# Means over heads by column tiles, squared once and spread by row tiles, in a two-layer convolution kernel

## The chip, the cores and the metric

The kernel runs on one core of one Trainium2 chip. The metric is the device time of one execution in microseconds (us). Ten runs of the kernel before took 4981.3 to 4992.86 us, median 4985.96. Engines: TensorE (PE; its weight loads are PEld), VectorE (DVE), ScalarE (ACT), GpSimd (POOL) and SyncE (SP), which only issues transfers here.

## The reference, cut to what matters

Layer 0 takes 32 images of 128 channels, 56 x 56 pixels: a depthwise convolution, a normalisation, and a mixture of eight experts of which each pixel uses two. Layer 1 then works on its result:

```python
feat = gelu(batchnorm(conv2d(x, conv_w, padding=3, dilation=3)))     # 64 channels
F2 = fft2(feat)
qkv = F2.reshape(B, 8 heads, 8 channels, N)
q = complex_l2_norm(qkv); k = complex_l2_norm(qkv); v = qkv
attn = einsum('bhdn,bhen->bhde', q, conj(k)) * tau
attn = complex(softmax(attn.real), softmax(attn.imag))
out_f = abs(ifft2(einsum('bhde,bhen->bhdn', attn, v)))
cg = sigmoid(conv1x1(gelu(batchnorm(conv1x1(F2.real)))))
gate = abs(ifft2(cg * F2))
return concatenate([out_f, gate], axis=1) + x
```

The kernel uses that out_f needs no transform at all: a matrix that mixes channels commutes with the transform, the real part of the attention acts on feat as a real 8 x 8 matrix per head, and the softmax of the imaginary part, which is constant, gives the mean over the eight channels of the head. So out_f is the root of (attn x feat) squared plus (mean over the head of feat) squared. That second term has only one row per head, but every channel of the head needs it.

## The kernel before, in words

Layer 0 ends with the experts; they write rows of `yf` in device memory. Layer 1 then goes over 16 pairs of images. The 128 partitions of a pair hold the 64 channels of one image and the 64 of the other, so there are 16 heads of 8 partitions.

Layer 0's result has still to be brought together for each pixel: 1568 indirect transfers, issued by POOL (line 400, in `release`), gather 128 rows of `yf` each into tiles `y` of seven (six buffers). When the 14 gathers of a row block are in, `total` (line 416) adds its two `y` to `xa` on DVE, writes the sum out on SP's queue, and `bring` (line 439) reads it back as `xs`. There are seven row blocks and so 98 gathers to a pair. A gather can start when its `y` has been added, and `y` is added where `total` stands in DVE's order. `worked(w)` sets that place: each piece of TensorE work reports its columns w, and one gather is asked for per `PACE` of them; `total` follows a block's last gather by seven. `bring` asks for whatever is still missing.

For a pair, `front` places the row blocks (`place`: seven transposes on PE, tile `pxs`, four additions on DVE, line 1174) and does the dilated convolution in seven groups of 8 rows (448 columns): `pf`, line 1185, nine taps in three steps of three, the two images side by side in two tiles of 64 columns. `back` does the rest: a forward transform of feat (tiles `pt`, `mid`, `pm`; line 1228 transposes, line 1215 copies, line 1236 multiplies), the attention matrix, the second forward transform into `Z`, then the stage that is edited, then two inverse transforms.

The edited stage: for each of the seven groups g, `attend(g)` multiplies feat by attn into a bank `pre` (line 1325) and by `meanw`, a 128 x 128 matrix with blocks of 1/8, into a bank `pim` (line 1326), so that each channel receives the mean of its head. ACT squares both (lines 1328 and 1329), DVE adds them back into feat (line 1330). Between the groups the gate is worked out: `pq` (line 1351, four column tiles of 32), and `pq2` (line 1363, four row tiles of 32 with a bank each), then the sigmoid (line 1369) and the product with Z on DVE (line 1374). `attended` takes the root later, between the steps of the inverse transform.

Banks: a pool of five serves `pre`, `pim`, `pq`, `pq2`, `pt`, `pm` and `pxs`; `pf` has two of its own.

Order: the front of the next pair is mixed into the back of this one by columns. After each piece of `back`, front steps are written until this goal is met:

```python
goal = max(0, made - LEAD) * FRONT // (MAIN - LEAD)
if w < 0:
    goal = max(goal, fed - w * 3 * 8 * W)
```

`made` counts the columns of back so far (a transform's step 64 per transpose and its output columns, an attend 896, each half of the gate 464), a front step counts 1344 (three taps) or 448 (a placed block), MAIN is 31304, FRONT 31360, LEAD a sixth of MAIN. A yield of -1 or -2 forces that many steps of taps. Over a pair back reports 27720 columns (MAIN also has 3584 of the gram matrix that are not reported), front 31360. The last pair has no front to mix in. On top of this, the framework's scheduler settles each engine's order when the program is built: by its own costs it pulls later work forward where it sees an engine waiting. The trace shows this where the taps of one step stand in pieces of two and four between `pt` and `pm`.

Of the kernel before, what the change touches and what calls it, by code (L numbers as in the profile page):

```python
# [30 lines left out]
F32 = mybir.dt.float32  # L31
I32 = mybir.dt.int32
AF = mybir.ActivationFunctionType
ALU = mybir.AluOpType
# [10 lines left out]
NT = H // 2  # L45
# [3 lines left out]
KF = 29  # L49
NPIX = H * W  # L50
P8 = 8
NB = H // P8
# [22 lines left out]
def conv_seq_kernel(ctx: ExitStack, tc: tile.TileContext, t: dict, out: bass.AP, dbg: dict):  # L75
    nc = tc.nc
# [14 lines left out]
    def bank(name):  # L91
        return psum.tile([128, 512], F32, tag="bank", name=name)

    def load(pool, name, shape, src, eng=None):
        s = pool.tile(shape, F32, name=name, tag=name)
        (eng or nc.sync).dma_start(out=s, in_=src)
        return s
# [24 lines left out]
    with tc.tile_pool(name="a1", bufs=1) as a1, tc.tile_pool(name="a2", bufs=2) as a2, tc.tile_pool(  # L122
        name="a4", bufs=4
    ) as a4, tc.tile_pool(
        name="a5", bufs=5
# [252 lines left out]
    step = {}  # L378
# [92 lines left out]
    if True:  # L471
# [39 lines left out]
        for u in range(U):  # L511
            nc.vector.tensor_scalar(
                out=blocks[:, u, :], in0=iota[:R, :NC], scalar1=float(-u), scalar2=None, op0=ALU.add
# [4 lines left out]
            out=token, in0=iota[:R], scalar1=-128.0, scalar2=lane[:R], op0=ALU.add, op1=ALU.add  # L518
# [601 lines left out]
    d1 = ctx.enter_context(tc.tile_pool(name="d1", bufs=1))  # L1120
    d2 = ctx.enter_context(tc.tile_pool(name="d2", bufs=2))
# [29 lines left out]
    gsc, gbi = batchnorm("cgbn")  # L1151
    tau = load(d1, "tau", [128, 1], t["tau"])
    neg = load(d1, "neg", [128, 128], t["neg"])
    meanw = load(d1, "meanw", [128, 128], t["meanw"])
    rw = load(d1, "rw", [2 * W, 4 * KF], t["rw"])
    rh = load(d1, "rh", [2 * H, 4 * KF], t["rh"])
    ih = load(d1, "ih", [4 * KF, 2 * H], t["ih"])
# [95 lines left out]
    def back(pr, xps, feat):  # L1253
# [56 lines left out]
        for i, w in enumerate(  # L1310
# [6 lines left out]
                parts[i]()  # L1317
            yield w

        def attend(g):  # L1320

            pre = bank("pre")
            pim = bank("pim")
            ftf = feat[:, 8 * g * W : 8 * (g + 1) * W]
            nc.tensor.matmul(pre[:, : 8 * W], lhsT=attn, rhs=ftf, start=True, stop=True)  # L1325
            step["pe"] = nc.tensor.matmul(pim[:, : 8 * W], lhsT=meanw, rhs=ftf, start=True, stop=True)
            sr = d2.tile([128, 8 * W], F32, name="sr")
            nc.scalar.activation(sr, pre[:, : 8 * W], AF.Square)
            nc.scalar.activation(pim[:, : 8 * W], pim[:, : 8 * W], AF.Square)
            nc.vector.tensor_tensor(out=ftf, in0=sr, in1=pim[:, : 8 * W], op=ALU.add)  # L1330
            return 2 * 8 * W

        def attended(g):

# [11 lines left out]
        NQ4 = NK * K2  # L1346
        starts = [min(q * NK, KF - NK) for q in range(4)]
        yield attend(0)
        pq = bank("pq")
        for q, k0 in enumerate(starts):  # L1350
            nc.tensor.matmul(
                pq[32 * q : 32 * (q + 1), :NQ4], lhsT=g1, rhs=Z[:, k0 : k0 + NK, :K2], start=True, stop=True,
                tile_position=(0, 32 * q),
# [3 lines left out]
        yield NQ4  # L1357
        for g in (1, 2, 3):
            yield attend(g)
        pq2 = [bank("pq2") for k0 in starts]  # L1360
        for q in range(4):
            p = slice(32 * q, 32 * (q + 1))
            nc.tensor.matmul(
                pq2[q][:, :NQ4], lhsT=g2[p, :], rhs=c1_[p, :], start=True, stop=True,
                tile_position=(32 * q, 0),
            )
        for q, k0 in enumerate(starts):
# [7 lines left out]
                out=zq, in0=zq, in1=gt[:, new:].broadcast_to([128, NK - new, 2, K2]), op=ALU.mult  # L1375
            )
        yield NQ4
        for g in range(4, NB):
            yield attend(g)
        yield -2  # L1380


# [34 lines left out]

    MAIN = 2 * (NT * (64 + 4 * KF) + KF * (64 + 4 * KF)) + NT * 128 + NB * 16 * W + 2 * -(-KF // 4) * 2 * KF  # L1420
    FRONT = NB * (NB * 64 + 9 * 8 * W)
    LEAD = MAIN // 6
    PACE = (MAIN + FRONT) / (2 * NP) * 1.07

# [6 lines left out]
    for pr in range(NI // 2):  # L1431
        then, steps = None, iter(())
        if pr + 1 < NI // 2:
            then = pair(pr + 1)
            steps = front(pr + 1, *then)
        made = fed = 0
        for w in back(pr, *this):
            made += max(w, 0)
# [3 lines that stand above are left out]
            worked(max(w, 0))  # L1442
            while fed < goal:
                f = next(steps, None)
                if f is None:
                    break
                fed += f
                worked(f)
        for w in steps:
            worked(w)  # L1450
        this = then


def constants(np):

    f = np.float32
    k = np.arange(KF)
    ang = 2 * np.pi * (np.outer(np.arange(H), k) % H) / H
    cos, sin = np.cos(ang), np.sin(ang)
    sin[:, 0] = 0  # L1460
    sin[:, KF - 1] = 0
    R = np.concatenate([cos, sin], 1)
    alpha = np.tile(np.where((k == 0) | (k == KF - 1), 1.0, 2.0), 2)
    inv = (R * alpha / H).T
    eye = np.eye(2)
    rw = np.kron(eye, R)

    both = np.array([[[1, 0], [0, -1]], [[1, 0], [0, 1]], [[0, 1], [1, 0]], [[0, -1], [1, 0]]])
    rh = np.einsum("hbl,xab->haxl", R.reshape(H, 2, KF), both)
    ih = np.einsum("blh,xab->xlah", inv.reshape(2, KF, H), both)  # L1470
    inw = inv.reshape(2, KF, W).transpose(1, 0, 2).reshape(2 * KF, W)
    iw = np.einsum("kw,ab->kabw", inw / 2, eye)
    blk = np.kron(np.eye(16), np.ones((8, 8)))
    p = np.arange(128)
    return {
        "ident": np.eye(128, dtype=f),
        "below": (p[:, None] < p[None, :]).astype(f),
        "lane": (FW * p).astype(f)[:, None],
        "revi": (E - np.arange(E)).astype(f),
        "neg": ((blk - 1) * BIG).astype(f),  # L1480
        "meanw": (blk / 8).astype(f),
        "eye2": np.tile(np.eye(DD), (2, 1)).astype(f),
        "rw": rw.astype(f),
        "rh": rh.reshape(2 * H, 4 * KF).astype(f),
        "ih": ih.reshape(4 * KF, 2 * H).astype(f),
        "iw": iw.reshape(4 * KF, 2 * W).astype(f),
    }
# [88 lines left out]
```

## Time and profile before

| what | value |
|---|---|
| median of ten runs | 4985.96 us |
| profiled execution, its own time | 4985.88 us |
| its span | 4984.1 us |
| layer 1's gathers, first to last | 2796.0 to 4859.5 us |
| first and last start of `pre` | 3110.4 and 4949.3 us |
| pre, pim (x112 each): busy | 109.2 and 102.6 us |
| squares, lines 1328 and 1329: mean of one | 544 and 529 ns |
| addition, line 1330: mean of one | 617 ns |

How to read it: in a line of a group, x is the number of instructions, then come busy us, the mean of one in ns, and idle time of the engine just before them with what ended it. A product of 32-bit numbers is two instructions. Products overlap in the array, so the mean of one is longer than what it adds to the chain; for a price the chain of waits is used, which gives the us that a group took from the chain's time. The windows view gives for each engine busy us and the number of instructions in a stretch.

### The profile page before, as it was taken

Reading aid. Unit: us, or ns where it says so; the run is one execution under the profiler, and the core shown is the slowest. Engines: PE = TensorE matmul, PEld = TensorE weight load, DVE = VectorE, ACT = ScalarE, POOL = GpSimd, SP = SyncE. Lnnn points to the kernel's source line nnn. Section 1 sums busy time; section 2 is a strip of 40 time slices with the busy share of each in tenths; the row PEclk is TensorE's granted clock in tenths of the full one; section 3 lists DMA queues with packets and bytes.
Section 4 is the critical chain, followed back from the end, with each engine's and each line's share of the span. In section 5 each row is a group of like instructions: output and inputs, shape, how many; then the busy total and the mean of one; then the engine's idle time right before and its main releaser. Section 6 shows DMA issues by size and latency. Waiting matters only on the chain.

```text
span 4984.1 us, 85712 instructions
## 1 busy us (share of the span) xinstructions
PE 4647.1 (93%) x32980; PEld 3187.3 (64%) x32980; DVE 2796.7 (56%) x5737; ACT 2175.4 (44%) x4258; POOL 2603.5 (52%) x2591
## 2 busy tenths in 40 slices
PE   7999984499989989899999999999999999999998
PEld 6676762376767667677777775665665666555556
DVE  4667668656575756673511223555555555555556
ACT  2666665144434444344555552333333333333334
POOL 0000002354525354567777477777777777777770
PEclk9998886699999999999999999999999999999999
DMA  9888873021212122123333666666666776666662
GB/s 244 233 251 228 235 217 95 21 71 55 71 45 73 54 64 63 57 67 91 98 103 108 198 174 154 180 180 185 184 173 172 187 189 190 178 180 185 183 164 60
DMA packets 767242, 705.13 MB, mean 141 GB/s; under 512 B 72751, under 2 KB 679088, under 8 KB 762740
## 3 DMA queue, kind: packets, MB, share of 16 engines
q1 hardware_dynamic: 596580, 487.54, 33.2%
q0 software_dynamic: 81664, 167.15, 14.4%
q10 hardware_dynamic: 88592, 44.96, 3.2%
q8 instruction: 262, 4.29, 0.4%
q14 instruction: 144, 1.18, 0.1%
HBM read 472.99 MB, written 226.39 MB: 140 GB/s over the span
## 4 chain that ended last, share of the span: by engine, by line
PE 67%; DVE 10%; issue 9%; POOL 7%; DMA 4%; ACT 2%; SPq 0%; DVEq 0%; POOLq 0%; ACTq 0%
PE pf L1185 14%; PE py L990 14%; PE ph L976 12%; PE pm L1236 8%; POOL y L400 4%; PE psa L157 4%; PE pt L1228 4%; POOL xg L953 3%; PE pyt L225 2%; PE pg L1260 2%; ACT y L208 2%; PE pxt L959 2%; DVE st L182 1%; PE pre L1325 1%; PE pxs L1170 1%
## 5 line engine op out<-in xcount | busy, mean ns | idle before, releaser
L400 POOL DMA_INDIRECT y<-yf,slot x1568 | 1567.0, 999 | 560.3 <-issue 438.8
L953 POOL DMA_INDIRECT xg<-xf,ids x861 | 886.0, 1029 | 835.7 <-DVE ids L878 308.6
L979 ACT ACTIVATE hT<-ph,b1t 128x512 f32<-128x512 f32 (+1 forms) x992 | 676.3, 682 | 1151.1 <-PE ph L976 1125.0
L990 PEld LDWEIGHTS py<-W,hT 128*128 128x128 f32 x7872 | 937.0, 191 | 145.6 <-issue 103.3
L990 PE MATMUL py<-W,hT 128*128 128x128 f32 x7872 | 984.4, 278 | 0.7
L976 PE MATMUL ph<-xT,W 128*128 128x512 f32 (+1 forms) x1984 | 895.3, 591 | 0.0
L1185 PE MATMUL pf<-xp,cw 128*64 128x448 f32 x4032 | 888.0, 549 | 0.3 <-DMA cgbn<-in_cgbn_dram 0.3
L1003 DVE TENSOR_TENSOR yo<-py,b2t 128x512 f32<-128x512 f32 (+2 forms) x256 | 170.3, 668 | 714.9 <-issue 563.3
L976 PEld LDWEIGHTS ph<-xT,W 128*128 128x128 f32 x1984 | 356.5, 192 | 332.5 <-issue 327.9
L1185 PEld LDWEIGHTS pf<-xp,cw 128*64 128x64 f32 x4032 | 276.7, 135 | 410.3 <-issue 373.4
L1215 DVE COPY mid<-pt 112x512 f32<-112x512 f32 (+3 forms) x480 | 308.4, 661 | 314.8 <-PE pt L1228 310.6
L214 POOL TENSOR_TENSOR y<-y,gB 128x2048 f32<-128x2048 f32 (+1 forms) x7 | 27.8, 3972 | 786.8 <-PE pyt L225 786.8
L208 ACT ACTIVATE y<-y,nb,sd 128x128 f32<-128x128 f32 x735 | 289.2, 481 | 97.1 <-DVE nb L195 97.1
L1013 ACT ACTIVATE yo<-yo,gates 128x128 f32<-128x128 f32 (+1 forms) x984 | 311.7, 390 | 9.6 <-DVE gates L878 5.7
L1239 ACT COPY T<-pm 128x464 f32<-128x464 f32 (+2 forms) x240 | 124.4, 520 | 375.8 <-PE pm L1236 375.7
L416 DVE TENSOR_TENSOR xa<-xa,y 128x896 f32<-128x896 f32 x224 | 243.2, 1086 | 56.2 <-DMA y<-yf,slot 52.1
L157 PE MATMUL psa<-xt,stay 112*64 112x98 f32 (+1 forms) x4608 | 250.4, 262 | 25.1 <-DMA stay<-in_wt_dram 18.5
L157 PEld LDWEIGHTS psa<-xt,stay 112*64 112x64 f32 (+1 forms) x4608 | 221.7, 145 | 76.1 <-issue 46.6
L165 DVE TENSOR_TENSOR y<-psa,dwbB 128x392 f32<-128x392 f32 x256 | 140.3, 555 | 162.5 <-PE psa L157 162.5
L1174 DVE SCALAR_TENSOR_TENSOR xp<-pxs,beta,xp 128x256 f32<-128x256 f32 x448 | 172.3, 444 | 96.7 <-PE pxs L1170 87.4
L225 PE MATMUL pyt<-ident,y 128*128 128x128 f32 x784 | 176.0, 332 | 53.8 <-ACT y L208 48.4
L959 PE MATMUL pxt<-ident,xg 128*128 128x128 f32 (+1 forms) x984 | 195.7, 278 | 24.4 <-DMA xg<-xf,ids 24.3
(401 smaller groups left out, 6106.9 us busy)
## 6 DMA issues: line engine op xcount, KB each, us to landing
xt<-in_x_dram SPq DMA_DIRECT2D x256, 392.0 KB
yf<-yo SPq DMA_DIRECT2D x240, 256.0 KB
xp<-in_xp_dram SPq DMA_DIRECT2D x32, 1832.0 KB
xa<-xf SPq DMA_DIRECT2D x112, 448.0 KB
xsum<-xa SPq DMA_DIRECT2D x112, 448.0 KB
xs<-xsum SPq DMA_DIRECT2D x112, 448.0 KB
xf<-y ACTq DMA_DIRECT2D x42, 1024.0 KB
y<-yf,slot POOLq DMA_INDIRECT x1568
```

Source lines behind the costliest of these rows:

```text
L157: nc.tensor.matmul(ps[h * 64 : (h + 1) * 64, c * TG : (c + 1) * TG], lhsT=wts[b][:, c4 + c, :], rhs=xv[: PKS[b], c, h, :, b * NB : b * NB ...
L208: nc.scalar.activation(yi, yi, AF.Identity, scale=sd[:, i : i + 1], bias=nb[:, i : i + 1])
L400: behind(nc.gpsimd.indirect_dma_start(out=begun_[r][1][-1][:, m, :], out_offset=None, in_=yf[: 1 + reach(r), :], in_offset=bass.IndirectOf ...
L953: behind(nc.gpsimd.indirect_dma_start(out=xg[:n, q, :], out_offset=None, in_=xf, in_offset=bass.IndirectOffsetOnAxis(ap=ids[:n, c0 + q : c ...
L959: nc.tensor.transpose(pt[:, q * 128 : q * 128 + n], xg[:n, q, :], ident[:n, :n])
L976: nc.tensor.matmul(ph[:, :ns], lhsT=W1[:, e, f * C : (f + 1) * C], rhs=xT[:, :ns], start=True, stop=True)
L979: gelu = nc.scalar.activation(hT[:, f, :ns], ph[:, :ns], AF.Gelu, bias=b1t[:, e, f : f + 1])
L990: nc.tensor.matmul(py[:n, q * C : (q + 1) * C], lhsT=hT[:, f, q * 128 : q * 128 + n], rhs=W2[:, e, f, :], start=(f == 0), stop=(f == FF // ...
L1013: nc.scalar.activation(yo[:n, q], yo[:n, q], AF.Copy, scale=gates[:n, c0 + q : c0 + q + 1])
L1185: step["pe"] = nc.tensor.matmul(pf[i * DD : (i + 1) * DD, : 8 * W], lhsT=cw[:, k, :], rhs=xps[i][:, o : o + 8 * RP].rearrange("p (h w) -> ...
L1215: step["dve"] = nc.vector.tensor_copy(to, of)
L1236: step["pe"] = nc.tensor.matmul(pm[:, i * M : (i + 1) * M], lhsT=mid[:m, i, :], rhs=by, start=True, stop=True)
```

## The change

`meanw` is replaced by `meanh` (128 x 32: one column per head, 16 of zeros) and `headb` (a 32 x 128 matrix that hands row h to the eight channels of head h, four times one below the other). An attend now multiplies feat by attn as before, and its four quarters of 112 columns (two rows of the image) by `meanh` in four column tiles. Each writes 32 partitions of one bank, in the columns of this group; the bank collects four groups, then three. ACT squares attn x feat straight into feat. `spread` then follows groups 0 to 3 and groups 4 to 6: ACT squares the collected means once (448 or 336 columns), four row tiles of 32 hand them to all channels, into a bank for each quarter, and DVE adds each quarter to feat. `MAIN` and the columns that the pieces report change with it: an attend 560, the spreads 448 and 336; MAIN becomes 29736, back's report 26152, and with them LEAD and PACE.

```diff
--- before.py
+++ after.py
@@ -1151,7 +1151,8 @@
     gsc, gbi = batchnorm("cgbn")
     tau = load(d1, "tau", [128, 1], t["tau"])
     neg = load(d1, "neg", [128, 128], t["neg"])
-    meanw = load(d1, "meanw", [128, 128], t["meanw"])
+    meanh = load(d1, "meanh", [128, 32], t["meanh"])
+    headb = load(d1, "headb", [128, 128], t["headb"])
     rw = load(d1, "rw", [2 * W, 4 * KF], t["rw"])
     rh = load(d1, "rh", [2 * H, 4 * KF], t["rh"])
     ih = load(d1, "ih", [4 * KF, 2 * H], t["ih"])
@@ -1317,18 +1318,49 @@
                 parts[i]()
             yield w
 
+        QW = 2 * W
+        means = {}
+
         def attend(g):
 
+            if g % 4 == 0:
+                means["p"] = bank("pim")
+            at = g % 4 * QW
             pre = bank("pre")
-            pim = bank("pim")
             ftf = feat[:, 8 * g * W : 8 * (g + 1) * W]
             nc.tensor.matmul(pre[:, : 8 * W], lhsT=attn, rhs=ftf, start=True, stop=True)
-            step["pe"] = nc.tensor.matmul(pim[:, : 8 * W], lhsT=meanw, rhs=ftf, start=True, stop=True)
-            sr = d2.tile([128, 8 * W], F32, name="sr")
-            nc.scalar.activation(sr, pre[:, : 8 * W], AF.Square)
-            nc.scalar.activation(pim[:, : 8 * W], pim[:, : 8 * W], AF.Square)
-            nc.vector.tensor_tensor(out=ftf, in0=sr, in1=pim[:, : 8 * W], op=ALU.add)
-            return 2 * 8 * W
+            for q in range(4):
+                step["pe"] = nc.tensor.matmul(
+                    means["p"][32 * q : 32 * (q + 1), at : at + QW],
+                    lhsT=meanh,
+                    rhs=ftf[:, q * QW : (q + 1) * QW],
+                    start=True,
+                    stop=True,
+                    tile_position=(0, 32 * q),
+                )
+            nc.scalar.activation(ftf, pre[:, : 8 * W], AF.Square)
+            return 10 * W
+
+        def spread(g0, ng):
+
+            n = ng * QW
+            sq = d1.tile([128, 4 * QW], F32, name="sq")
+            nc.scalar.activation(sq[:, :n], means["p"][:, :n], AF.Square)
+            ps = [bank("pim") for q in range(4)]
+            for q in range(4):
+                p = slice(32 * q, 32 * (q + 1))
+                step["pe"] = nc.tensor.matmul(
+                    ps[q][:, :n], lhsT=headb[p, :], rhs=sq[p, :n], start=True, stop=True, tile_position=(32 * q, 0)
+                )
+            fv = feat[:, 8 * g0 * W : 8 * (g0 + ng) * W].rearrange("p (g q w) -> p g q w", g=ng, q=4)
+            for q in range(4):
+                nc.vector.tensor_tensor(
+                    out=fv[:, :, q, :],
+                    in0=fv[:, :, q, :],
+                    in1=ps[q][:, :n].rearrange("p (g w) -> p g w", g=ng),
+                    op=ALU.add,
+                )
+            return n
 
         def attended(g):
 
@@ -1357,6 +1389,7 @@
         yield NQ4
         for g in (1, 2, 3):
             yield attend(g)
+        yield spread(0, 4)
         pq2 = [bank("pq2") for k0 in starts]
         for q in range(4):
             p = slice(32 * q, 32 * (q + 1))
@@ -1377,6 +1410,7 @@
         yield NQ4
         for g in range(4, NB):
             yield attend(g)
+        yield spread(4, NB - 4)
         yield -2
 
 
@@ -1417,7 +1451,7 @@
 
 
 
-    MAIN = 2 * (NT * (64 + 4 * KF) + KF * (64 + 4 * KF)) + NT * 128 + NB * 16 * W + 2 * -(-KF // 4) * 2 * KF
+    MAIN = 2 * (NT * (64 + 4 * KF) + KF * (64 + 4 * KF)) + NT * 128 + (12 * NB) * W + 2 * -(-KF // 4) * 2 * KF
     FRONT = NB * (NB * 64 + 9 * 8 * W)
     LEAD = MAIN // 6
     PACE = (MAIN + FRONT) / (2 * NP) * 1.07
@@ -1478,7 +1512,8 @@
         "lane": (FW * p).astype(f)[:, None],
         "revi": (E - np.arange(E)).astype(f),
         "neg": ((blk - 1) * BIG).astype(f),
-        "meanw": (blk / 8).astype(f),
+        "meanh": np.pad(blk[:, ::8] / 8, ((0, 0), (0, 16))).astype(f),
+        "headb": np.tile(np.pad(blk[::8], ((0, 16), (0, 0))), (4, 1)).astype(f),
         "eye2": np.tile(np.eye(DD), (2, 1)).astype(f),
         "rw": rw.astype(f),
         "rh": rh.reshape(2 * H, 4 * KF).astype(f),
```

## The prediction

> **What bounds the kernel now.** I read the page's busy shares first, then the windows view cut at each pair of images of layer 1, then the gathers' own waits, last the chain over one pair. The page:
>
> ```profile
> PE 4647.1 (93%) x32980; PEld 3187.3 (64%) x32980; DVE 2796.7 (56%) x5737; ACT 2175.4 (44%) x4258; POOL 2603.5 (52%) x2591
> ...
> L400 POOL DMA_INDIRECT y<-yf,slot x1568 | 1567.0, 999 | 560.3 <-issue 438.8
> ```
>
> TensorE looks like the only bound, POOL half idle. But the gathers of line 400 run only from 2796.0 to 4859.5, and those 2063.5 us are their 1567.0 busy plus 496.6 of the 560.3 idle (63.7 lie before the first one). Of that, 438.8 us are the fixed 0.305 between two gathers. So POOL is as full as TensorE. Windows per pair (length, PE, PEld, DVE, ACT, POOL busy, clock, DMA share, GB/s):
>
> ```profile
> 3354.70:3473.80 119.10, 119.10 (x746) 72.93 (x746) 71.25 (x121) 44.01 (x74) 91.50 (x91) 1.00 0.70 188
> 3473.80:3594.00 120.20, 120.20 (x746) 73.19 (x747) 69.37 (x119) 44.13 (x74) 92.16 (x93) 1.00 0.68 182
> 3594.00:3715.30 121.30, 121.30 (x746) 73.53 (x747) 69.17 (x119) 44.16 (x74) 85.14 (x87) 1.00 0.62 173
> ...
> 4200.00:4321.40 121.40, 121.40 (x746) 73.34 (x746) 71.06 (x121) 44.09 (x74) 93.37 (x93) 1.00 0.69 187
> 4321.40:4448.40 127.00, 123.59 (x746) 74.28 (x747) 71.28 (x121) 44.24 (x74) 97.44 (x98) 0.99 0.65 182
> ```
>
> To 4321 TensorE never idles, and a pair uses 98 gathers while POOL makes 91 to 93; the lead it began with is eaten up. Then four pairs take 126 to 129 us, the time of 98 gathers at 1.30, and TensorE idles 12.8 us in them. The end is set by the gathers, then the 124.5 us behind the last one. TensorE's pace reaches the gathers in one place, where POOL waits for line 416 to free a buffer (gathers in 3600 to 4000):
>
> ```profile
> its engine sat idle before it (us, times) until:
>   issue: 80.7, 265
>   DVE xa L416: 20.4, 11
> ```
>
> Less 11 plain gaps that is 17.0 us, in pairs 5 to 7 (the 87 above). Line 416 stands there in VectorE's order by work done, so a faster TensorE frees the buffers sooner: at most 17 us are to be had, however much TensorE saves. The edited stage on the chain (start, us):
>
> ```profile
> 3349.72 0.76 PE pre L1325 x2
> 3350.49 0.75 PE pim L1326 x2
> 3351.24 2.41 PE pf L1185 x12
> 3353.65 0.92 PE pq L1351 x8
> 3354.56 0.95 PE pre L1325 x2
> 3355.51 0.75 PE pim L1326 x2
> ...
> 3365.05 0.99 PE pq L1363 x8
> 3366.04 2.41 PE pf L1185 x12
> ```
>
> **The change, part by part** (profiled execution: 4985.88 us, 4984.1 span and 1.8 around it; the median of the runs is 4985.96).
>
> *Means.* Removed: 7 products pim, 0.75 each, 5.25 us a pair, all on the chain. Added: 7 groups of four 32-column tiles with 112 columns each. pq is the same form with 464 columns: its four tiles run side by side, 0.92 against 0.75 x 464/448 = 0.777 for one tile's stream, so 0.147 fixed. 112 columns stream in 0.187; a group is 0.33. Bounds: 0.19 (nothing fixed) and 0.88 (four in a row, as pm's 0.22 each for 112 to 116 columns, 0.88 for its x8 on the chain). I take 0.33, from the row with the same tiles.
>
> *Spreads.* Added: row tiles over 448 and 336 columns, like pq2 (0.99 for 464, so 0.217 fixed): 0.75 + 0.56 streamed. The first stands ahead of pq2, so the two share one change of shape.
>
> *Changes of shape.* pre is 0.75 after a full product and 0.95 after tiles; pf's step is 2.24 of streams (three taps, halves side by side) and 2.41 shown. Going through the order of a pair with these (0.15 to 0.22 a change) I count 34 changes before and 43 after: +1.6 us. Bound below: 0.
>
> *Order.* An attend counts 560 instead of 896, a spread 448 or 336, so the front steps fall elsewhere. By the fill rule, from pre3 on: before, pre3 pim3, pf2.0, pq2, pf2.1, pre4 pim4, pf2.2, pre5 pim5, pre6 pim6, place 4, pf3.0, pf3.1, pf3.2, T4's transposes. After, pre3 mean3, pf2.0, spread, pq2, pf2.1, pre4 mean4, pre5 mean5, pf2.2, pre6 mean6, spread, place 4, pf3.0, pf3.1, transposes, pf3.2 among them.
>
> Sum for TensorE, streams and changes: -5.25 + 7 x 0.187 + 1.31 + 1.6 = -1.05 us a pair. Without any price for changes -2.6; with the four in a row 7 x (0.88 - 0.33) = 3.8 worse, +2.8.
>
> The Trainium skill, TensorEngine Tiling (Array Packing), Tiling Modes, says that a change of mode drains TensorE, with no figure; it speaks against this edit, and the 0.95 beside 0.75 agrees. By the rule alone the nine changes cost something unknown, by the rows 1.6 us.
>
> *ScalarE.* 14 squares of 0.53 to 0.55 become 9; it is at 44 of 120 us. Nothing on the path. The square in place must now wait for the mean products that read feat, 0.33 later; it covers nothing.
>
> *VectorE.* 7 additions of 0.617 become 4 of 0.617 and 4 of about 0.49: 4.3 against 4.4 us. Both forms read one operand from PSUM; in the rows gathers beside L1330 last 0.95 as elsewhere, so POOL loses nothing. What changes is that they come four at a time.
>
> *Waits added.* Spread's TensorE work waits for two ScalarE operations behind the last mean: 0.2 + 0.55 + 0.53 + 0.2 = 1.5 us. For the first, pf2.0 (2.41) lies between and hides it; if the planner puts pf2.0 elsewhere it costs 1.5. For the second nothing lies between in written order: 0 if the planner pulls in place 4 or pf3.0, else 1.4. Then pq2: five banks, four held by the spread until its additions have read them, one free. Three of pq2's products wait for three additions, 3 x 0.62 + 0.3 = 2.2 us; hidden if pf2.1 is pulled ahead (the chain shows pf pulled in pieces between pt and pm elsewhere), else paid, and behind them in TensorE's queue stand pre4 and all that follows. Uncovered 0 to 3.6 us a pair (the means' bank is held over four attends, leaving four for place and pre; that is inside this). I take 0.6, since the planner fills with pf wherever it sees a wait: net -0.45 us a pair, bounds -2.6 and +2.55.
>
> The skill's same page, PSUM Bottleneck, warns that tiling speeds up TensorE and not the reading of PSUM. Here four banks filled in 0.96 us take VectorE 2.5; by the rule the additions decide and 2.2 us are lost, by my sum a quarter of that.
>
> *Queues.* SP: one load more (meanw's issue took 0.328 us at 3015.2, first use at 3110): 0 to 0.33, hidden. POOL: pace is 667.1 for 684.2 and work per pair 57,512 for 59,080, so 86.22 gathers asked per pair instead of 86.35; 0.13 x 1.3 = 0.2 us a pair later in the paced stretch, and no step of either queue is passed by another.
>
> *The gathers.* About five pairs lie before the 17 us of waits: 5 x 0.45 = 2.3 us come back. Later pairs wait for gathers anyway; what TensorE saves there goes into idle time.
>
> *Behind the last gather.* Two terms. pf3.2 stood before the stall at 4859 (the 36 pf run until it) and now stands behind: 0 to +2.4, I take 2. The last pair has no front to hide in: 13.7 us from pre0 (4936.83) to T4's transposes (4950.57). After: 1.09 + 0.77 + 3 x 1.28 = 5.7, wait 1.5, spread 0.96, pq2's last at 10.2 and done at 11.1, 3 x 1.28: 14.95, so +1.2; if the transposes also stand behind the second spread, +2.1 more, and the additions delay mid by up to 1.2. Bounds +1.2 and +4.5, I take 2.5.
>
> Sum: 4985.9 - 2.3 + 2 + 2.5 = 4988.
>
> **The rivals.** 0.2% is 10 us, about what a measurement of this kernel tells from nothing.
> - *Hand-over uncovered (slower).* All 3.6 us of waits are paid: 3.6 - 1.05 = 2.55 a pair, 5 x 2.55 = 12.8, with the tail's 4.5 gives 5003. It decides from a net loss of 1.1 us a pair. For it: four additions in a row on a VectorE that also has place's four (1.6 us) and line 416 (1.08) there. Against: no wait of TensorE in ten pairs today.
> - *Saving paid in full (faster).* Changes of shape cost nothing, waits hidden: 5 x 2.6 = 13 back of the 17, tail +1: 4974. For it: POOL's waits on L416. Against: 0.95 beside 0.75.
> - *Another order.* Pairs of one program differ by 2.3 us (119.1 to 121.5) with equal work, by where the pieces of pf fall. Five pairs at 2.3 are 11.5 either way: 4976 or 5000.
> - *The tiles don't run side by side.* +2.8 a pair and 2 us for the first spread, over 5 pairs 24, and the tail 6: 5016. pq's row speaks against it.
>
> **How the numbers follow.** Forecast, the end held by the gathers with small terms, 0.45 (own range 4979 to 4995); hand-over 0.23; full saving 0.12; another order 0.08 each way; no overlap 0.04. Faster 0.12 + 0.08 = 0.20, same 0.45, slower 0.23 + 0.08 + 0.04 = 0.35. The range goes from the full saving to just past the hand-over, 4974 to 5006, and leaves out the case without overlap and half of the outer ends.
>
> **What would show it.** Right: a group of means near 0.33 on the chain, first spread near 0.96, pre behind a mean 0.95; fewer than 17 us of POOL waiting for L416 in pairs 5 to 7; the gathers end within 6 us of 4859.5; last gather to end 127 to 130 us. Wrong: TensorE idle in the first ten pairs waiting for the additions at pq2 (hand-over); pairs at 117 (full saving); mean groups near 0.88; or a gather longer than 0.945 beside the new additions, which would lengthen POOL's chain and which no row shows.

## The result, and the profile after

The changed kernel takes 5001.95 us (median of 9 runs) beside 4986.31 (median of 30 runs of the kernel before): 1.0036 times as long, 95% interval 1.0027 to 1.0045. That is slower by 16 us, just where the hand-over rival stood (5003), and 14 above the forecast of 4988. The page of the changed kernel:

```profile
span 5001.5 us, 87461 instructions
...
PE 4670.2 (93%) x33908; PEld 3173.0 (63%) x33908; DVE 2794.5 (56%) x5753; ACT 2175.7 (44%) x4208; POOL 2599.5 (52%) x2591
...
L400 POOL DMA_INDIRECT y<-yf,slot x1568 | 1566.9, 999 | 575.2 <-issue 441.9
```

The gathers' own 1566.9 us and their mean of 999 ns have not moved: additions four at a time do not hold POOL up. What moved is TensorE's pair. Windows from gate to gate, the same columns as before:

```profile
3228.60:3350.00 121.40, 121.30 (x804) 72.93 (x805) 68.98 (x120) 44.22 (x70) 92.87 (x94) 1.00 0.69 184
3350.00:3471.30 121.30, 121.20 (x804) 72.85 (x805) 70.91 (x122) 44.22 (x70) 92.77 (x91) 1.00 0.67 183
...
4210.40:4333.80 123.40, 123.30 (x804) 73.40 (x805) 70.73 (x122) 44.33 (x71) 94.72 (x95) 1.00 0.68 187
...
4582.10:4710.90 128.80, 126.59 (x804) 75.24 (x805) 70.70 (x122) 44.32 (x70) 98.92 (x99) 0.97 0.65 179
```

In the early pairs 119 to 120 us became 121.4, in the late ones 121.4 became 123.3. In the first three windows TensorE shows no idle time, because a product that waits inside a group is counted with the group; the last has 2.2 us of it, in which TensorE waits behind the gathers. The chain has the waits (start, us):

```profile
3355.79 0.75 PE pre L1331 x2
3356.54 0.33 PE pim L1333 x8
3356.87 2.41 PE pf L1186 x12
3359.28 0.96 PE pim L1352 x8
3360.24 2.80 PE pq L1396 x8
3363.04 2.41 PE pf L1186 x12
3365.45 0.95 PE pre L1331 x2
...
3371.36 0.33 PE pim L1333 x8
3371.69 2.40 PE pf L1186 x10
3374.09 0.78 PE pim L1352 x8
3374.87 1.12 PE pxs L1171 x7
3375.99 3.15 PE pf L1186 x14
```

pq2, 0.99 before, takes 2.80 right behind the first spread; place's transposes, 0.77 or 0.92 elsewhere, take 1.12 right behind the second. Means (0.33) and spreads (0.96 and 0.78) cost what they were expected to. What pq2 waits for stands at its weight loads (PEld):

```profile
3360.93 0.29 PEld L1396 LDWEIGHTS pq<-c__27692,g 32*128 32x128 f32 x2 [0.69 <-DVE feat L1357]
3361.46 0.29 PEld L1396 LDWEIGHTS pq<-c__27692,g 32*128 32x128 f32 x2 [0.24 <-DVE feat L1357]
3361.99 0.29 PEld L1396 LDWEIGHTS pq<-c__27692,g 32*128 32x128 f32 x2 [0.24 <-DVE feat L1357]
```

Line 1357 is the spread's addition. Three loads wait, each for one addition, 0.53 us apart; over the 16 pairs there are 48 such waits.

Summed over the second pair (before from 3235.5, after from 3228.6), the chain's groups differ by: pim, all forms, 5.25 to 4.05; pq and pq2 together 1.91 to 3.71; pf 52.48 to 53.35; pxs 5.37 to 5.87; pre 6.63 to 6.83; the rest within 0.1. That is -1.20 + 1.80 + 0.87 + 0.50 + 0.20 = +2.17 us a pair.

The whole time can be laid out by the 16 starts of the gate's gelu. "Own pairs" is the time between the first and the last start, less "stretch": what the last four full pairs are longer than an undisturbed late pair of that kernel (121.4 before, 123.3 after), which is time spent behind the gathers.

| us | to first gelu | own pairs | stretch | from last gelu | span |
|---|---|---|---|---|---|
| before | 3115.5 | 1801.4 | 23.3 | 43.9 | 4984.1 |
| after | 3107.2 | 1833.7 | 10.6 | 50.0 | 5001.5 |
| after, step between (e1) | 3113.9 | 1801.0 | 25.7 | 47.0 | 4987.6 |
| before, more PE (e3) | 3110.3 | 1831.1 | 12.8 | 47.5 | 5001.7 |
| before, pace 1.03 (e4) | 3110.3 | 1801.8 | 9.3 | 45.3 | 4966.7 |
| after, pace 1.03 (e12) | 3104.2 | 1842.3 | 0.4 | 49.7 | 4996.6 |

The first column is almost all work that no edit touches; it differs by 11 us between single executions (the changed kernel's gathers start at 2787.0 instead of 2796.0, so its 8 us lie ahead of layer 1). The second says it: 32 us in 15 pairs, 2.15 a pair on average, which is the 2.17 of the chain. The third gives 13 of them back. From the first gelu on, the changed kernel's profiled execution took 25.7 us more, and the shorter way to it hides 8.3 of them.

### The profile page after: what moved, and what is told of

Read it like the earlier page. It is cut to its first block, busy times and chain, and to the rows that moved or that the text cites. A ratio compares the mean times of both kernels' runs of the same rounds, so it can differ in the third digit from the quotient of the medians.

```text
span 5001.5 us, 87461 instructions
## 1 busy us (share of the span) xinstructions
PE 4670.2 (93%) x33908; PEld 3173.0 (63%) x33908; DVE 2794.5 (56%) x5753; ACT 2175.7 (44%) x4208; POOL 2599.5 (52%) x2591
## 4 chain that ended last, share of the span: by engine, by line
PE 70%; DVE 10%; issue 8%; POOL 5%; DMA 3%; ACT 3%; SPq 0%; DVEq 0%; POOLq 0%; ACTq 0%
PE pf L1186 16%; PE py L990 13%; PE ph L976 12%; PE pm L1237 8%; PE pt L1229 4%; PE psa L157 4%; POOL xg L953 3%; ACT y L208 2%; POOL y L400 2%; PE pg L1261 2%; PE pre L1331 2%; PE pyt L225 2%; PE pxs L1171 2%; PE pxt L959 2%; DVE st L182 1%
## 5 line engine op out<-in xcount | busy, mean ns | idle before, releaser
L400 POOL DMA_INDIRECT y<-yf,slot x1568 | 1566.9, 999 | 575.2 <-issue 441.9
L1186 PE MATMUL pf<-xp,cw 128*64 128x448 f32 x4032 | 901.4, 551 | 0.3 <-DMA g2b<-in_cg_b_dram 0.3
```

Of the source, the lines that this page charges most:

```text
L400: behind(nc.gpsimd.indirect_dma_start(out=begun_[r][1][-1][:, m, :], out_offset=None, in_=yf[: 1 + reach(r), :], in_offset=bass.IndirectOf ...
L1186: step["pe"] = nc.tensor.matmul(pf[i * DD : (i + 1) * DD, : 8 * W], lhsT=cw[:, k, :], rhs=xps[i][:, o : o + 8 * RP].rearrange("p (h w) -> ...
```

## The experiments

The theory after the result (A): pq2 waits for banks that the spread's additions hold; TensorE's loss reaches the end through line 416, in the paced pairs only. Rivals: the loss is in the changes of shape; or TensorE sets the end in all pairs.

**Step between (e1).** In the changed kernel, a front step forced between spread and pq2:

```diff
         yield spread(0, 4)
+        yield -1
         pq2 = [bank("pq2") for k0 in starts]
```

> The changed kernel with one front step of three taps forced between the first spread and pq2 (the step that came right after pq2), 2.41 us of TensorE work that needs no bank of the pool. Theory A (pq2's 2.80 us on the chain instead of 0.99 is its wait for the banks that the spread's additions hold): pq2 back near 1.0, pairs from 121.4 to about 119.6, and because TensorE's pace reaches the gathers only in the first five or six pairs, 5002 - 5.5 x 1.8 = 4992. If TensorE set the end in all pairs: 5002 - 15 x 1.8 = 4975. Rival B (the loss is in the changes of shape and not in the banks): no change, 5002. Rival C (the wait moves to pre, which then needs a bank that pq2 holds until the sigmoid): 5000 to 5002, with pre4 above 2 us.

Measured 4982.79 us beside 4986.9 for the kernel before on the same chip, 0.9992 [0.9983, 1.0001]. The chain of this kernel:

```profile
3362.49 0.96 PE pim L1352 x8
3363.46 2.41 PE pf L1186 x12
3365.87 0.99 PE pq L1397 x8
3366.86 0.95 PE pre L1331 x2
...
3375.55 0.78 PE pim L1352 x8
3376.32 1.12 PE pxs L1171 x7
```

pq2 is back at 0.99 with the same instructions in the same shapes, so the 1.8 us was a wait and not the tiles (rival B falls), and the wait didn't move to pre (C falls: 0.95). The 1.12 behind the second spread, left alone, stays. The pairs are as long as before the change (119.6), own pairs 1801.0 against 1801.4. The time fell by 19 and not by the 10 that A had for this run, nor by the 27 of all pairs without the gathers: the first hint that A has the path wrong.

**No means (e2).** In the kernel before, the product by meanw left out, so that the output lacks the mean's part:

```diff
-            pim = bank("pim")
-            step["pe"] = nc.tensor.matmul(pim[:, : 8 * W], lhsT=meanw, rhs=ftf, start=True, stop=True)
...
-            nc.scalar.activation(pim[:, : 8 * W], pim[:, : 8 * W], AF.Square)
-            nc.vector.tensor_tensor(out=ftf, in0=sr, in1=pim[:, : 8 * W], op=ALU.add)
+            nc.scalar.activation(pre[:, : 8 * W], pre[:, : 8 * W], AF.Square)
+            nc.vector.tensor_tensor(out=ftf, in0=sr, in1=pre[:, : 8 * W], op=ALU.add)
```

> The kernel before without the products by meanw; the addition takes the square of pre twice, so the mean's part of the output is left out. All columns that are reported, and so the pace of the gathers, stay as before; TensorE has 5.25 us a pair less to do. Theory A (the end is set by the gathers, of which TensorE can give back the 17 us that POOL waits for line 416): POOL's waits on line 416 near zero in pairs 5 to 7, pairs first near 114, then about 128, last gather about 17 us earlier, and 3 to 5 us less in the last pair: 4962 to 4972. Rival (TensorE sets the end): 4986 - 16 x 5.25 = 4902.

Measured 4961.21 us, 0.995 [0.9937, 0.9963]. 84 us of TensorE work gone (16 x 5.25), 26 us gained. POOL's waits of this kernel (us in total, times, longest):

```profile
POOL y L400 <- issue: 439.9, 1442, 0.7
POOL y L400 <- DMA xg<-xlast: 64.2, 1, 64.2
...
POOL y L400 <- DVE xa L416: 2.7, 9, 0.3
```

Nine plain gaps are left of the waits on line 416. The gathers run for 2044.1 us instead of 2063.5, the early pairs take 114 to 118 and six late ones 126 to 130. So the gathers hold the end near 4960, just under the range that A gave: 84 us less for TensorE shorten them by 19 us.

**More TensorE work (e3).** In the kernel before, pim's product made twice in three of seven groups:

```diff
-            step["pe"] = nc.tensor.matmul(pim[:, : 8 * W], lhsT=meanw, rhs=ftf, start=True, stop=True)
+            for again in range(2 if g in (1, 3, 5) else 1):
+                step["pe"] = nc.tensor.matmul(pim[:, : 8 * W], lhsT=meanw, rhs=ftf, start=True, stop=True)
```

> The kernel before with the product by meanw made twice in groups 1, 3 and 5: 3 x 0.75 = 2.25 us more TensorE work a pair, nothing else changed. This prices what an excess like that of the changed kernel (about 2 us a pair) costs in all. Theory A: five or six pairs count, the rest goes into time in which TensorE would wait for gathers: 5.5 x 2.25 = 12.4 and 2.25 in the last pair, 5001. Rival (TensorE sets the end): 16 x 2.25 = 36, 5022. Rival (nothing but the last pair counts): 4988.

Measured 5003.32 us, 1.0036 [1.0023, 1.0048], like the changed kernel. This met A's 5001, but for another reason, as the table shows: own pairs grew by 29.7, which is 2.1 to 2.4 in each of the first ten (the fifteenth, and last, is 2 us shorter), and the stretch behind the gathers shrank by 10.5. Not five pairs count, but all of them, less what the wait for the gathers shrinks. By the total alone the two could not be told apart here.

**Earlier gathers, before (e4).** In the kernel before, one number:

```diff
-    PACE = (MAIN + FRONT) / (2 * NP) * 1.07
+    PACE = (MAIN + FRONT) / (2 * NP) * 1.03
```

> The kernel before with the factor of PACE at 1.03 instead of 1.07: 89.7 gathers asked for per pair instead of 86.35, TensorE's work unchanged. Theory A (POOL's 17 us of waits come from where line 416 stands in VectorE's order): the waits on line 416 vanish in pairs 5 to 7, the last gather ends 10 to 17 us earlier, 4970 to 4976. Rival (TensorE sets the end): 4986. Rival (line 416 then stands ahead of its gathers and holds up VectorE in the first pairs): 4990 or more.

Measured 4966.76 us, 0.996 [0.9947, 0.9973]. As A had it, and 3 us below its range: the waits on line 416 are 2.7 us in 9 plain gaps, the gathers 2049.8 us long, the stretch 9 us instead of 23, own pairs unchanged (1801.8). This beats both kernels by a line that has nothing to do with the means: 20 us of the kernel before were lost because gathers were asked for too late in pairs 5 to 7 and missed at the end.

**Earlier gathers, after (e5, e9, e12).** The same line in the changed kernel; three runs, because the first two fell on chips where the kernel before took 6237 and 6220 us.

> The changed kernel with the factor of PACE at 1.03 instead of 1.07; the banks and the order of TensorE's work as in the change. Theory A (the 2 us a pair that pq2 waits reach the end only because they delay line 416 in the paced pairs): pq2 still near 2.8 on the chain, the waits on line 416 (35.9 us in the changed kernel, some 7 of it plain gaps) nearly gone, gathers 2050 us long instead of 2080, time 5002 - 29 = 4973, within 4969 and 4980. Rival (TensorE's own waits are on the path in all pairs): 5002 less a few us.

> The changed kernel with the factor of PACE at 1.03 again, on a chip that runs the kernel before in its usual time (about 4986). Theory A (the 2 us a pair that pq2 waits reach the end only because they delay line 416 in the paced pairs): pq2 still near 2.8 on the chain, the waits on line 416 (35.9 us in the changed kernel, some 7 of it plain gaps) nearly gone, gathers 2050 us long instead of 2080, time 5002 - 29 = 4973, within 4969 and 4980. Rival (TensorE's own waits are on the path in all pairs): 5002 less a few us.

> The changed kernel with the factor of PACE at 1.03, for a chip that runs the kernel before in about 4986. Theory A (the 2 us a pair that pq2 waits reach the end only because they delay line 416 in the paced pairs): pq2 still near 2.8 on the chain, the waits on line 416 (35.9 us in the changed kernel, some 7 of it plain gaps) nearly gone, gathers 2050 us long instead of 2080, time 4969 to 4980. Rival (TensorE's own waits are on the path in all pairs): 5002 less a few us.

Measured on a chip with 4984.7 for the kernel before: 5002.41 us, 1.0037 [1.0023, 1.005]. Nothing gained, where the kernel before gained 20. This refutes A, and the rival that it had on record, TensorE's own waits on the path in all pairs, gave 5002 less a few us. Windows of this kernel, each a pair:

```profile
3227.50:3356.60 129.10, 126.34 (x804) 74.07 (x805) 68.91 (x120) 44.22 (x70) 98.83 (x99) 0.97 0.65 173
3356.60:3478.10 121.50, 121.40 (x804) 73.02 (x805) 71.02 (x122) 44.02 (x70) 93.45 (x93) 1.00 0.69 187
...
4586.90:4710.20 123.30, 123.20 (x804) 73.22 (x804) 70.74 (x122) 44.25 (x70) 94.35 (x93) 1.00 0.69 185
4710.20:4833.80 123.60, 123.50 (x804) 73.45 (x805) 70.75 (x122) 44.33 (x71) 94.69 (x94) 1.00 0.65 173
```

The late pairs are 123.3 and 123.6, no longer 126 to 129: the stretch behind the gathers is gone (0.4). But for the first two pairs TensorE now works without a gap to the last pair, and its 15 pairs of 2.15 us too much stand in the time in full: 32 us more than the 4966.76 of the kernel before at this pace would be 4999. POOL's waits on line 416 are still 28.5 us, 20 of them now after 3849: with TensorE as the bound it is POOL that has time to spare. Some 8 us went to one early pair (129.1). The chain there waits 2.62 us for a gather's data, then come line 416 (1.09), the spread's first addition, and pq2: an addition that TensorE needs back stands in VectorE's order behind a line 416 that still waits for its gathers. Without that the run might have come out some 8 us shorter, and still far from 4973.

On the two other chips the changed kernel at this pace took 0.9906 [0.9888, 0.9925] and 0.9842 [0.9814, 0.987] of the kernel before. There POOL waits 931 and 926 us for line 416 and a pair takes 164 to 202 us; in the second of them (e9) TensorE is busy for 306 of the 400 us from 3500 to 3900, at a mean granted clock of 0.86, where the kernel before on its usual chip has 400 at 1.00. What holds it up the records don't show (26% of the chain there is put down to "another core or an unknown queue"). These times cannot be set beside the others, and they are not.

**Step and pace (e6, e10).** Both edits in the changed kernel.

> The changed kernel with the front step between the first spread and pq2 and the factor of PACE at 1.03. Theory A: with the pace out of the way TensorE's 2 us a pair no longer matter; what is left of the hand-over is the last pair, so the time is that of the changed kernel with the pace alone or up to 8 us less: 4965 (4983 less the 18 us of waits on line 416), and level with the kernel before at the same pace (4967). Rival (the 19 us that the step brought are TensorE's and add to the pace's): 19 us below the changed kernel with the pace alone.

> The changed kernel with the front step between the first spread and pq2 and the factor of PACE at 1.03, again on such a chip. Theory A: with the pace out of the way TensorE's 2 us a pair no longer matter; level with the kernel before at that pace (4967), 4963 to 4969, and at most 8 us below the changed kernel with the pace alone. Rival (the 19 us that the step brought are TensorE's and add to the pace's): 19 us below the changed kernel with the pace alone.

Both ran on those chips: 6162.7 us, 0.9889 [0.9871, 0.9908], and 6136.44 us, 0.9863 [0.9835, 0.989]. Against the changed kernel with the pace alone (0.9906, 0.9842) that is a little less once and a little more once. pq2 has no wait in any pair of e10 but the last, which has no front. What the two edits give together on a chip with the usual time wasn't measured.

**More TensorE work and pace (e7).**

> The kernel before with the mean's product made twice in groups 1, 3 and 5 (2.25 us more TensorE work a pair) and the factor of PACE at 1.03. At the factor 1.07 these products cost 16 us. Theory A: with gathers asked for early enough only the last pair's 2.25 us and what TensorE can't hide behind the gathers remain: 4967 to 4973, beside 4966.8 for the kernel before at the same pace. Rival (TensorE's work adds up over the pairs): 4967 + 16 = 4983 or more.

On the first of those chips: 6256.79 us, 1.0032 [1.0013, 1.005] of the kernel before there. It doesn't answer the question.

**Six banks (e8, e11).** In the changed kernel, the gram product's bank put into the pool:

```diff
-    psum = ctx.enter_context(tc.tile_pool(name="psum_d", bufs=5, space=PSUM))
+    psum = ctx.enter_context(tc.tile_pool(name="psum_d", bufs=6, space=PSUM))
-    psum1 = ctx.enter_context(tc.tile_pool(name="psum_g", bufs=1, space=PSUM))
-        pg = psum1.tile([128, 128], F32, name="pg")
+        pg = bank("pg")[:, :128]
```

> The changed kernel with six banks in the pool instead of five: the gram product takes its bank from the pool instead of a pool of its own, and gives it back before the edited stage. Theory A (pq2 waits for banks, one for each addition): with two banks free beside the spread's four, pq2 waits for two additions of 0.62 us instead of three, so its 2.80 us on the chain become about 2.2, and place's transposes behind the second spread fall from 1.12 to about 0.95; some 0.8 us a pair, 5.5 pairs: 4997. Rival (pq2 waits for the additions as such, whatever the banks): 2.80 as before, 5002.

> The changed kernel with six banks in the pool instead of five, the gram product's bank taken from the pool, again on such a chip. Theory A (pq2 waits for banks, one for each addition): pq2's 2.80 us on the chain become about 2.2, and place's transposes behind the second spread fall from 1.12 to about 0.95; some 0.8 us a pair, 5.5 pairs: 4997. Rival (pq2 waits for the additions as such, whatever the banks): 2.80 as before, 5002.

6156.47 us, 0.9877 [0.9852, 0.9903], and 6115.93 us, 0.9822 [0.9803, 0.9842], on the same two chips, so the expected 4997 is untested. The length of pq2 can be read all the same, since it is the wait of one group for VectorE. TensorE's timeline of the changed kernel (a group from its first start to its last end, which is some 0.1 to 0.2 more than its share of the chain):

```profile
3359.21 1.03 PE L1352 MATMUL pim<-sq,headb 32*128 32x448 f32 x8
3360.06 2.97 PE L1396 MATMUL pq<-c__27692,g 32*128 32x464 f32 x8
```

and with six banks:

```profile
3481.42 1.03 PE L1351 MATMUL pim<-sq,headb 32*128 32x448 f32 x8
3482.27 2.44 PE L1395 MATMUL pq<-c__25660,g 32*128 32x464 f32 x8
```

2.97 became 2.44 in 11 of the 16 pairs of e8, but in only 7 of 16 of e11; the others are longer, some of them at about half the clock (a product of 976 ns for 547). With five banks on the first of these chips 2.97 stands in 14 of 16 (e5). One more bank takes away 0.53 us, the distance from one addition to the next in the weight loads above. So pq2 waits for banks, one addition for each.

## Why the prediction was right, and where it was not

The range (4974 to 5006) held the time, and the rival that came is the one it named, with its place (pq2 behind the spread) and its price (5003 for 5002); that the price fits so closely is luck, as the third point shows. The forecast took the other side of it, and three steps failed:

- *"I take 0.6, since the planner fills with pf wherever it sees a wait."* Measured: 1.80 at pq2 and, after the second spread, some 0.2 to 0.35 at place. The planner left pq2 right behind the spread (the chain shows no pf between). It did fill where it was expected to before both spreads: no wait of 1.4 or 1.5 us shows there. The additions decide, as the Trainium skill has it (TensorEngine Tiling (Array Packing), PSUM Bottleneck): 1.80 of the 2.2 us that the rule made of it were lost.
- *"-1.05 us a pair."* Without the waits it came to nothing: e1's pairs are as long as those before the change. The parts that were counted held: means 0.33, spreads 0.96 and 0.78, 0.95 for a pre after tiles. What was missed is pf: +0.87, for which the sum had nothing but changes of shape. In two places of a pair the planner cut two steps into 10 and 14 instructions: 2.40 and 3.15 us, together 5.55, where two steps of 12 are 4.82 (2 x 2.41). Both cuts are +1.46; longer runs elsewhere give some of it back. x10 costs as much as x12 (2.41), and x14 0.74 more: a tap cut between its two images takes its whole stream twice.
- *"About five pairs lie before the 17 us of waits"*, and later pairs wait anyway. Wrong: what TensorE loses counts in all 15 pairs, less what the waits behind the gathers can give. 2.15 x 15 = 32 us were added to own pairs, and 13 of the 23 us behind the gathers went away for them. I had counted the waits at 4321 to 4830 as slack of any size; they were 23 us in all, and 15 pairs of 2.15 are more than that. Nor did all 23 go: the gathers took 2079.7 us instead of 2063.5, since POOL waited longer for line 416 (31.3 us between 3560 and 4000, where it was 20.7), and the forecast had this wait get shorter. On the chain that ended last the gathers still take 1.9% of the span, where they took 4.2%. The rival's price was right by luck: 2.55 x 5 = 12.8 stands for 32.3 - 12.7 = 19.6 and its tail of 4.5 for 6.1, and the 8.3 us less before the first gelu, which the change has no part in, bring the profiled execution to +17.4.

The tail: +6.1 from the last gelu (forecast +2.5, at most +4.5), and +4 between the last gather and that gelu (forecast +2, at most +2.4). In the last pair the wait at pq2 came as worked out, but TensorE also slowed down, as the last section shows: pre took 1.79 instead of 0.95 twice. The kernel with the step between has the same last pair without the slowing and shows +3.1, near the forecast. The +4 is more than the step of pf that was worked out: the chain holds 5.7 us more of pf there and less waiting. It does not pass the last gather any more, but leaves the gathers 20 us earlier, again through line 416 and an addition of the spread, and goes on in TensorE's work of that pair:

```profile
4846.76 2.69 DMA y<-yf,slot
...
4849.62 1.09 DVE xa L416
4850.72 0.54 DVE feat L1357
...
4851.30 2.92 PE pq L1396 x6
```

Confirmed: the gathers as a floor (e2), 17 us of POOL's waits to be had (e2 shortened the gathers by 19, and e4 gained 20), no longer gathers beside the additions, and ScalarE off the path in the pairs that have a front (44.2 us busy in 121). A single change of shape cost what the rows said (their sum over a pair, 1.6 us, was not measured by itself); the Trainium skill's rule that a change of mode drains TensorE (same page, Tiling Modes) agrees with 0.95 beside 0.75 in this kernel's chain too.

## What to carry to other kernels

Where two chains of nearly equal length share a kernel, a price on one is not multiplied by the few places where they touch today: work out both chains to the end, with the new price in each pair, and take the longer. Four results that come out at once need as many buffers as the reader takes to read them and the next work needs to start; a step that needs none of them, put between in writing, is worth more than one bank more. A result that one engine needs back from another also waits for whatever stands ahead of it in that other engine's order. A planner that fills waits fills those that its own costs show it, and that is to be seen from the order it writes, not assumed.

## What the runs showed of the hardware that was not expected

The granted clock of TensorE fell in the last pair, during pq2 and after the wait at the spread (1.05 us without work of TensorE). Windows of the changed kernel around it:

```profile
4940.00:4956.00 16.00, 14.17 (x125) 9.85 (x124) 5.06 (x13) 10.80 (x19) 0.00 (x0) 1.00 0.00 1
4956.00:4966.00 10.00, 10.00 (x42) 3.20 (x37) 6.08 (x8) 4.11 (x7) 0.00 (x0) 0.66 0.00 0
```

and the chain there:

```profile
4956.32 3.53 PE pq L1396 x8
4959.85 1.79 PE pre L1331 x2
4961.64 0.53 PE pim L1333 x8
4962.17 1.79 PE pre L1331 x2
```

In windows of 1 us the clock is 1.00 up to 4958, 0.63 in the next, 0.50 from 4959 to 4965 and 1.00 from 4966. Some 3 us are lost (3.53 for 2.80, twice 1.79 for 0.95, twice 0.53 for 0.33, and 1.26 for a third pre). The same kernel at the pace of 1.03 shows 3.67 and 1.79 in this place; the one with the step between, which has the same waits in its last pair, shows 2.80 and 0.95. What decides it these runs don't tell.

On the chips where the kernel before takes 6220 to 6237 us, every variant of the changed kernel (with the other pace, the step or six banks) was 1 to 2% faster than the kernel before, and the kernel before with more TensorE work and the other pace 0.3% slower. The changed kernel as it stands was not run there, nor the kernel before at that pace alone. The change may suit such a chip; whether and why it does stays open. The mean granted clock of a whole execution is 0.88 to 0.89 there and 0.95 to 0.96 on the others, with every kernel.
